# Four accumulators of an attention unit: the order of their matmuls in the first and the last pair of source blocks

## The chip, the cores and the metric

The kernel runs on one core of a Trainium2 chip. The metric is the device time of one execution in microseconds (us); lower is better. TensorE is called PE in the profile, VectorE DVE, ScalarE ACT, GpSimd POOL and SyncE SP.

## The reference

Four graph layers run one after the other over 4096 nodes with 64 features and one dense 0/1 adjacency. Each is wrapped as `x = x + layer(relu(layernorm(x)), adj, ...)`. The change lies in the first layer, a graph attention with eight heads of width 32. Its core is, cut to what matters:

```
mask = (adj > 0)
e    = leaky_relu(f1[:, None] + f2[None, :], 0.2)        # one per head
h    = elu(softmax(where(mask, e, -9e15)) @ Wh)          # 4096x4096 times 4096x32
```

Six heads are "spatial" (f1 and f2 come from the node features), two are "intent" heads (f1 and f2 come from an embedding). The heads' outputs are joined, multiplied by `W_out`, and a ninth attention of the same form follows; then the other three layers.

## The kernel before

**What a unit computes.** exp(leaky_relu(s + t)) takes one of two forms, by the sign of s + t, and each form is a product of a factor of the target and a factor of the source. So a head needs no exponential per edge: the kernel makes, for each edge, the flag "s + t is positive" (B) and "an edge where it isn't" (C), as bytes that TensorE reads as 8-bit floats, and sums the sources' scaled values over B and over C. A unit is one head over one half of the targets (2048 of 4096). There are 2 x 8 = 16 units, in the order of halves and, within them, of heads. They take the time from about 48 to 935 us of the profile.

**What a unit's loop does.** The 4096 sources are 32 blocks of 128; the loop at line 1552 and on takes them in 16 pairs. For each pair, `split_edges` makes the signs `st` of two blocks (line 1205 on ScalarE, or line 1199 on VectorE for a part of them), then B (line 1211, VectorE, an AND with the edges), then C (line 1219, VectorE, a XOR) where the pair is not "whole". In a whole pair the edges themselves take C's place, and B's share is taken off by a second set of matmuls with negated values `ycn`. The first and the last pair of a spatial unit are not whole; nor is the first pair of an intent unit.

**Accumulators.** Each product of one block is four matmuls, on four groups of 32 columns of TensorE, into four groups of 32 partitions of one accumulator (`add_up`, line 1541). The accumulators are PSUM tiles of 128 x 512 float32:

- accB: the values over B (two or three parts: a spatial head has one half-precision part here and its low part in accL; an intent head has three parts in accB)
- accL: the low part of a spatial head's values over B
- accD: the denominators over B
- accC: the values over C

accB and accC alternate between two pools from head to head (`ps_acc` and `ps_acc2`), so a unit's own pair of them is free while the one before is emptied. accL and accD are one tile each, in `ps_acc`: a unit can't write them before the unit before has been emptied.

**The end of a unit.** After the loop, eight small matmuls (line 1649) add a correction to accC, and then the four are emptied into `ev` (part of `h`): accD by VectorE (line 1657), accB by ScalarE (line 1658), accC by ScalarE (line 1659), and for spatial heads accL by VectorE (line 1661), which adds accL to what line 1658 has written and so waits for it. What follows from `ev` (`finish_unit`: transposes at line 1676, division, and after four heads the product with `W_out`) is put off to the third and fourth source block of the next unit.

**What sets the order.** The code issues the instructions in the order in which it is written, and the framework that compiles it places them into each engine's queue by priority (earlier in the code comes first) among those that its own estimate holds to be ready. So the queue's order is near the code's order and not the same. [...] B tiles are three deep, C and `st` tiles two deep. Inside a pair the code before emits, for each of the two blocks, accB, accL (spatial heads), accD; then for each block accC. In the first unit of each half (head 0) further matmuls into `dm` are tied behind the last of these products (`behind(sums)`), and in the very first unit the products of the other heads (`other_products`) too.

Of the kernel before, what the change touches and what calls it, by code (L numbers as in the profile page):

```python
# [26 lines left out]
NB = N // P  # L27
D = 64
G = 512
# [806 lines left out]
def kernel(  # L836
# [204 lines left out]
    with ExitStack() as l0:  # L1041
# [99 lines left out]
        def transfers_after(src, *pairs):  # L1141

            ins = nc.gpsimd.tensor_copy(tick.bitcast(src.dtype)[:, 0 : src.shape[1]], src)
            with tc.issue_after(ins.ins):
                for dst, s in pairs:
                    nc.gpsimd.dma_start(dst, s)
# [29 lines left out]
        @contextmanager  # L1176
        def behind(*marks):

            with ExitStack() as e:
                for i in marks:  # L1180
                    e.enter_context(tc.issue_after(i))
                yield
# [118 lines left out]
        with ExitStack() as pa:  # L1301
# [49 lines left out]
            with in_order():  # L1351
                nc.vector.tensor_reduce(fsum, FT[0:F, :], AX.X, ALU.add)
                for b0 in range(0, NB, 8):
                    pw = (ps, ps2)[b0 // 8 % 2].tile([P, 8, KZ], F32, name="pst", tag="misc")
                    for b in range(8):
# [4 lines left out]
                            start=True,  # L1360
                            stop=True,
# [50 lines left out]
                for k in range(2):  # L1412
                    pr = ps.tile([P, G], F32, name="prs", tag="misc")
                    for q in range(4):
# [5 lines left out]
                            start=True,  # L1420
                            stop=True,
# [23 lines left out]
        with ExitStack() as ha:  # L1445
# [27 lines left out]
            def load_products(zt, hd):  # L1473
                src = Z_d.rearrange("k p (h i) -> p k h i", h=NH - 1)[:, :, hd - 1, :]
                nc.sync.dma_start(zt.rearrange("p (k b) o -> p k (b o)", b=4), src)
# [4 lines left out]
            for hf in range(2):  # L1480
# [9 lines left out]
                for hd in range(NH):  # L1490
                    first = hd == 0
# [26 lines left out]
                    elif hf == 0 or hd + 1 < NH:  # L1518
# [6 lines left out]
                    spatial = hd < HS  # L1525
                    ycn = hp.tile([P, NB, 2 * O], F16, name="ycn", tag="ycn")
                    nc.vector.tensor_scalar(ycn, yc, -1.0, None, ALU.mult)
                    accB, accC = (
                        (ps_acc, ps_acc2)[hd % 2].tile([P, G], F32, name=n, tag=n)
                        for n in ("accB", "accC")  # L1530
                    )
                    accL, accD = (ps_acc.tile([P, G], F32, name=n, tag=n) for n in ("accL", "accD"))

                    parts = [(accB, yb[:, c]) for c in range(3)]
                    if spatial:
                        parts = [(a, yb[:, c].bitcast(F16)) for c, a in enumerate((accB, accL))]
                    parts.append((accD, yb[:, len(parts)]))

                    def add_up(acc, values, moving, start, stop):
                        for k in range(NS):  # L1540
                            ins = nc.tensor.matmul(  # L1541
                                acc[k * O : (k + 1) * O, :],
                                lhsT=values,
                                rhs=moving(k),
                                start=start,
                                stop=stop,
                            )
                        return ins.ins
# [3 lines left out]
                    for j0 in range(0, NB, 2):  # L1552
                        q = j0 // JT
                        t0 = j0 % JT
                        if spatial:
                            whole = j0 // 2 % 3 > 0
                        else:
                            whole = j0 // 2 % (5 if hf else 2) == 1
                        edges = mres[q][:, t0 : t0 + 2, :]
                        B, C = split_edges(  # L1560
                            epool,
                            srow,
                            nt[:, j0 : j0 + 2, hd],
                            edges,
                            j0 + hd * NB,
                            HEAD_STEPS[not spatial],
                            not whole,
                            3,
                        )
                        if whole:  # L1570
                            C = edges.bitcast(F8)
                        for i, j in enumerate(range(j0, j0 + 2)):
                            for n, (acc, y) in enumerate(parts):
                                sums = add_up(
                                    acc,
                                    y[:, j],
                                    lambda k, i=i: B[:, i, k * G : (k + 1) * G],
                                    start=j == 0 and (n == 0 or acc is not parts[n - 1][0]),
                                    stop=j == NB - 1 and (acc is not accB or n == len(parts) - 2 - spatial),
                                )  # L1580
                        for i, j in enumerate(range(j0, j0 + 2)):
                            for c in range(2):
                                cs = slice(c * O, (c + 1) * O)
                                add_up(
                                    accC,
                                    yc[:, j, cs],
                                    lambda k, i=i: C[:, i, k * G : (k + 1) * G],
                                    start=j == 0 and c == 0,
                                    stop=False,
                                )  # L1590
                                if whole:
                                    add_up(
                                        accC,
                                        ycn[:, j, cs],
                                        lambda k, i=i: B[:, i, k * G : (k + 1) * G],
                                        start=False,
                                        stop=False,
                                    )
                            if first:
                                with behind(sums):  # L1600
                                    add_up(
                                        dm,
                                        YD[:, j].rearrange("p c h -> p (c h)"),
                                        lambda k, q=q, j=j: mres[q].bitcast(F8)[
                                            :, j % JT, k * G : (k + 1) * G
                                        ],
                                        start=(j == 0),
                                        stop=(j == NB - 1),
                                    )
                        if hf == 0 and hd > 0 and j0 % (NB // 2) == 8 and later:  # L1610
                            transfers_after(B.bitcast(U8)[0:1, 0, 0:4], *later.pop(0))
                        if hf == 0 and first and j0 // 2 < NB // 4:
                            with behind(sums, *done_at):
                                other_products(j0 // 2)
                        if hf == 0 and first and j0 == NB // 2:
                            load_products(zt, hd + 1)
                        if j0 >= (NB // 2 + 4 if first else NB // 2 - 4):
                            with behind(*done_at):
                                for _ in range(2 if first else 1):
                                    next(coming, None)  # L1620
                        if j0 == 2 and pending:
                            pending()
                            pending = None
                    if first:
# [4 lines left out]
                        for b in range(GB):  # L1629
# [4 lines left out]
                                start=True,  # L1634
                                stop=True,
# [11 lines left out]
                    for c in range(2):  # L1647
                        for k in range(NS):
# [4 lines left out]
                                start=False,  # L1653
                                stop=c == 1,
# [254 lines left out]
        with ExitStack() as ob:  # L1909
# [185 lines left out]
            for u in range(4):  # L2095
                us = slice(u * HO2, (u + 1) * HO2)
                hs = slice((u % 2) * HO2, (u % 2 + 1) * HO2)
                accB, accC = (
                    [ps_acc.tile([P, G], F32, name="acco", tag="acc") for _ in range(NK)]
                    for _ in range(2)  # L2100
                )

                dd = ps_acc.tile([P, G], F32, name="ddo", tag="acc")
                for q in range(NQ):
# [11 lines left out]
                    for t in range(0, JT, 2):  # L2116
                        j0 = q * JT + t
                        edges = m[:, t : t + 2, :]
                        whole = j0 // 2 % 4 == 1
                        B, C = split_edges(  # L2120
                            work, srow[:, us], nto[:, j0 : j0 + 2], edges, j0, NB + 1, not whole, 4
                        )
# [6 lines left out]
                        for acc, Y, E in products:  # L2129
                            for i in range(2):  # L2130
                                for k in range(NK):
                                    sums = nc.tensor.matmul(
                                        acc[k],
                                        lhsT=Y[:, i].rearrange("p s d -> p (s d)"),
                                        rhs=E[:, i, k * G : (k + 1) * G],
                                        start=j0 + i == 0,
                                        stop=acc is accB and j0 + i == NB - 1,
                                    )
                    with behind(sums.ins):
                        for t in range(JT):  # L2140
                            j = q * JT + t
# [32 lines left out]
                for k in range(NK):  # L2174
# [4 lines left out]
                        start=False,  # L2179
                        stop=True,  # L2180
# [707 lines left out]
```

## Time and profile before

| | |
|---|---|
| median of 3 runs | 2041.64 us (2033.41 to 2043.93) |
| the profiled execution | 2039.13 us, of it 2037.1 us span |
| heads, 16 units | 48 to 935 us of the span |
| a unit in the second to the sixteenth place | 46 to 67 us, most 48 to 58 |
| TensorE's granted clock | mean 0.938 |

By units, from the changes of unit as the copies of accB show them (busy us of each engine; the first row is the unit of head 1 in the first half):

| stretch, us | length | PE | DVE | ACT | PE clock |
|---|---|---|---|---|---|
| 137 to 190 | 53 | 50.57 | 46.95 | 44.07 | 0.94 |
| 190 to 241 | 51 | 48.08 | 48.11 | 45.20 | 0.97 |
| 241 to 298 | 57 | 48.06 | 51.24 | 47.90 | 0.97 |
| 298 to 356 | 58 | 55.64 | 49.28 | 47.61 | 0.94 |
| 411 to 466 | 55 | 53.83 | 50.55 | 52.46 | 0.97 |
| 631 to 679 | 48 | 46.70 | 45.42 | 43.17 | 1.00 |
| 732 to 788 | 56 | 53.17 | 45.76 | 45.59 | 0.97 |
| 889 to 935 | 46 | 45.78 | 41.46 | 37.61 | 1.00 |

How to read it: a row of the profile's groups gives line, engine, operation, output and inputs, shape and count, then busy us and mean ns of one, and behind the second bar the engine's idle time just ahead of these instructions with what ended most of it. A row of the waits gives who waited for whom, the total us, how often, and the longest. A row of the timeline gives start, length, engine, line and operation, and in brackets the idle time ahead of it with its releaser. A row of the stretches gives the stretch, its length, each engine's busy time with its count of instructions (PE, PE's weight loads, DVE, ACT, POOL), the granted clock of TensorE, the DMA share and GB/s. The four matmuls of one product overlap, so their busy times are not a sum.

### The profile page before, as it was taken

To read this page: it belongs to the slowest core of one execution; us is meant where nothing else is said; L and a number is where in the kernel's file an instruction comes from. 1 tells how busy PE (TensorE), PEld (TensorE's weight loads), DVE (VectorE), ACT (ScalarE), POOL (GpSimd) and SP (SyncE) were. 2 spreads that over 40 slices of the span, in tenths; PEclk is the share of its full clock that TensorE was granted. 3 is DMA by queue.
4 is the path that set the end of the run, shared out by engine and by line. 5 is a ranking of instruction groups with operands and counts; after the bars stand their busy time and mean duration, and the time that the engine had idled before them with its cause. 6 is when DMAs were issued, how large, how long until landed. Compare 5 with 4: busy or idle time off the path is not lost. (4 is left out here: it accounts for less than half of the span.)

```text
span 2037.1 us, 44155 instructions
## 1 busy us (share of the span) xinstructions
PE 1815.8 (89%) x19323; PEld 821.8 (40%) x19340; DVE 1530.0 (75%) x2239; ACT 1476.9 (72%) x1439; POOL 83.3 (4%) x125
## 2 busy tenths in 40 slices
PE   5889989999999999996788958999999995789998
PEld 3444445444444444443234442333333333344332
DVE  5779988998789879996989867888788788533000
ACT  2768987899689878993778847777777753227676
POOL 2000100100000000001011100000000000000000
PEclk8899999999999999997899977999999996899999
DMA  9945555434211111103686406444344334412232
GB/s 112 178 115 99 100 99 72 164 118 172 86 49 49 48 49 54 54 2 125 254 276 227 163 17 235 137 145 143 124 140 140 124 134 151 152 63 70 91 99 64
DMA packets 117016, 239.05 MB, mean 117 GB/s; under 512 B 11062, under 2 KB 84006, under 8 KB 102054
## 3 DMA queue, kind: packets, MB, share of 16 engines
q1 hardware_dynamic: 101996, 192.95, 28.1%
q0 software_dynamic: 14816, 43.18, 11.8%
q8 instruction: 153, 2.51, 0.5%
q14 instruction: 51, 0.42, 0.1%
HBM read 245.37 MB, written 49.46 MB: 145 GB/s over the span
## 5 line engine op out<-in xcount | busy, mean ns | idle before, releaser
L1205 ACT ACTIVATE st<-srow,nt 128x2048 int8<-128x2048 f32 x352 | 682.8, 1994 | 78.9 <-DVE B L1211 78.1
L1211 DVE TENSOR_TENSOR B<-st,mres 128x1024 int32<-128x1024 int32 x256 | 311.7, 1220 | 70.5 <-PE accC L1541 46.6
L1541 PE MATMUL accB<-B,ybh 128*32 128x512 fp8e4 x3072 | 340.6, 384 | 13.3 <-DVE B L1211 13.3
L1541 PE MATMUL accD<-B,ybh 128*32 128x512 fp8e4 x2048 | 303.0, 388 | 23.0 <-DVE h L1657 23.0
L1541 PEld LDWEIGHTS <-ybh 128*32 128x32 bf16 (+1 forms) x6656 | 197.4, 98 | 236.8 <-issue 74.8
L1541 PE MATMUL accC<-mres,ych 128*32 128x512 fp8e4 x2272 | 269.2, 381 | 0.0
L1541 PE MATMUL accC<-B,ycn 128*32 128x512 fp8e4 x2272 | 269.0, 381 | 0.0
L1541 PE MATMUL accL<-B,ybh 128*32 128x512 fp8e4 x1536 | 221.6, 390 | 4.6 <-DVE h L1661 4.5
L1541 PEld LDWEIGHTS <-ych 128*32 128x32 f16 x4096 | 170.2, 99 | 116.1 <-issue 11.3
L1199 DVE TENSOR_SCALAR st<-srow,nt 128x2048 uint8<-128x2048 f32 x160 | 205.4, 1284 | 2.5
L2339 PE MATMUL accj<-sg,who 128*64 128x512 f32 (+1 forms) x512 | 197.8, 616 | 5.9 <-DVE sg L2332 5.5
L2339 PE MATMUL acci<-sg,who 128*64 128x512 f32 (+1 forms) x512 | 197.8, 616 | 0.0
L2295 ACT ACTIVATE yt<-pu,consts 128x512 f32<-128x512 f32 x144 | 98.7, 687 | 98.7 <-PE pu L2294 98.6
L2284 ACT ACTIVATE sg<-pl,rb 128x512 f32<-128x512 f32 x256 | 160.9, 679 | 8.2 <-PE pl L2279 5.2
L2771 ACT ACTIVATE w3b<-pv 128x1024 int16<-128x1024 f32 x128 | 131.0, 1024 | 42.4 <-PE pv L2762 41.2
L1205 ACT ACTIVATE st<-srowo,nto 128x1024 int8<-128x1024 f32 x128 | 138.3, 1138 | 25.0 <-DVE B L1211 24.9
L1541 PE MATMUL accC<-C,ych 128*32 128x512 fp8e4 x1824 | 149.3, 393 | 0.8 <-DVE C L1219 0.8
L955 DVE SCALAR_TENSOR_TENSOR raw<-raw 128x2048 f32<-128x2048 f32 x64 | 146.1, 2282 | 3.3 <-DMA raw<-in_adj_dram 3.3
L1219 DVE TENSOR_TENSOR C<-B,mres 128x1024 int32<-128x1024 int32 x114 | 139.5, 1225 | 3.6
L1541 PEld LDWEIGHTS <-ycn 128*32 128x32 f16 x2272 | 108.4, 97 | 62.7 <-issue 1.9
L2332 DVE SCALAR_TENSOR_TENSOR sg<-pf,sg 128x512 f32<-128x512 f32 x112 | 72.1, 685 | 38.9 <-PE pf L2329 38.9
L2778 DVE COPY ev<-sacc 128x512 f32<-128x512 f32 x4 | 2.8, 691 | 124.8 <-PE sacc L2736 124.8
(497 smaller groups left out, 2756.4 us busy)
## 6 DMA issues: line engine op xcount, KB each, us to landing
raw<-in_adj_dram SPq DMA_DIRECT2D x64, 1024.0 KB, 6.0
mo<-edges SPq DMA_DIRECT2D x32, 512.0 KB, 4.9
noedge<-nmo POOLq DMA_DIRECT2D x32, 512.0 KB, 4.3
nm<-noedge SPq DMA_DIRECT2D x64, 256.0 KB, 3.1
m<-edges SPq DMA_DIRECT2D x16, 1024.0 KB, 4.8
m<-edges SPq DMA_DIRECT2D x32, 512.0 KB, 3.8
srow<-srow_d SPq DMA_DIRECT2D x15, 1024.0 KB, 6.7
mres<-in_adj_dram POOLq DMA_DIRECT2D x8, 1024.0 KB, 35.4
```

What stands on the lines that cost most here:

```text
L955: nc.vector.scalar_tensor_tensor(raw, raw, 0.0, raw, ALU.is_gt, ALU.not_equal, accum_out=bad[:, c : c + 1])
L1199: nc.vector.tensor_scalar(st[:, i, :].bitcast(U8), srow, negs[:, i : i + 1], EDGE, ALU.is_gt, ALU.mult)
L1205: nc.scalar.activation(st[:, i, :], srow, AF.Sign, bias=negs[:, i : i + 1], scale=-1.0)
L1211: nc.vector.tensor_tensor(B.bitcast(I32), st.bitcast(I32), edges.bitcast(I32), ALU.bitwise_and)
L1219: nc.vector.tensor_tensor(C.bitcast(I32), B.bitcast(I32), edges.bitcast(I32), ALU.bitwise_xor)
L1541: ins = nc.tensor.matmul(acc[k * O : (k + 1) * O, :], lhsT=values, rhs=moving(k), start=start, stop=stop,)
L2284: nc.scalar.activation(sg[:, b0 + k, :], pl, AF.Sigmoid, bias=rb[:, j : j + 1], scale=1.0)
L2295: nc.scalar.activation(far[gi, gj][:, b, :], pu, AF.Sigmoid, bias=nb_t, scale=2.0 * DIST_K / (DIST_S * DIST_S),)
L2332: nc.vector.scalar_tensor_tensor(v[:, t, :], pf, F_K3, v[:, t, :], ALU.add, ALU.mult)
L2339: nc.tensor.matmul(acc[r : r + n, :], lhsT=XQ[:, src, cols], rhs=w, start=start, stop=stop)
L2771: nc.scalar.activation(w, pv, AF.Relu)
L2778: (nc.vector.tensor_copy if k % 2 else nc.scalar.copy)(ev[:, k, :], accs[k])
```

## The change

Inside the loop over pairs, the products over B are split into those into accB and those into the others (accL and accD). In the last pair of every unit, those into accL and accD of both blocks come first, then those into accB of both blocks, then accC as before. In the first pair of every unit but the two of head 0, those into accB of both blocks come first, then accC of both blocks, and those into accL and accD of both blocks last. All other pairs keep their order. The instructions themselves, their operands and their number stay as they are.

```diff
-                        for i, j in enumerate(range(j0, j0 + 2)):
-                            for n, (acc, y) in enumerate(parts):
-                                sums = add_up(
-                                    acc,
-                                    y[:, j],
-                                    lambda k, i=i: B[:, i, k * G : (k + 1) * G],
-                                    start=j == 0 and (n == 0 or acc is not parts[n - 1][0]),
-                                    stop=j == NB - 1 and (acc is not accB or n == len(parts) - 2 - spatial),
-                                )
+                        def inside(of_b):
+                            for i, j in enumerate(range(j0, j0 + 2)):
+                                for n, (acc, y) in enumerate(parts):
+                                    if (acc is accB) not in of_b:
+                                        continue
+                                    ins = add_up(
+                                        acc,
+                                        y[:, j],
+                                        lambda k, i=i: B[:, i, k * G : (k + 1) * G],
+                                        start=j == 0 and (n == 0 or acc is not parts[n - 1][0]),
+                                        stop=j == NB - 1
+                                        and (acc is not accB or n == len(parts) - 2 - spatial),
+                                    )
+                            return ins
+
+                        if j0 == NB - 2:
+                            inside([False])
+                            sums = inside([True])
+                        elif j0 == 0 and not first:
+                            sums = inside([True])
+                        else:
+                            sums = inside([True, False])
...
+                        if j0 == 0 and not first:
+                            inside([False])
                         if hf == 0 and hd > 0 and j0 % (NB // 2) == 8 and later:
```

## The prediction

> **What bounds the kernel now.** I read the page first: TensorE is the busiest engine, VectorE and ScalarE are close, and line 1541, which issues the products of the heads, holds the largest matmul rows.
>
> ```profile
> PE 1815.8 (89%) x19323; PEld 821.8 (40%) x19340; DVE 1530.0 (75%) x2239; ACT 1476.9 (72%) x1439; POOL 83.3 (4%) x125
> ...
> L1541 PE MATMUL accB<-B,ybh 128*32 128x512 fp8e4 x3072 | 340.6, 384 | 13.3 <-DVE B L1211 13.3
> L1541 PE MATMUL accD<-B,ybh 128*32 128x512 fp8e4 x2048 | 303.0, 388 | 23.0 <-DVE h L1657 23.0
> ```
>
> The idle time ahead of accD is not a lack of data: line 1657 is the copy that empties accD of the unit before. Then the waits of TensorE from 137 to 935 us, the heads after their first unit:
>
> ```profile
> PE accD L1541 <- DVE h L1657: 19.7, 10, 3.9
> PE pt L1676 <- DVE rd L1693: 7.4, 7, 2.1
> PE accL L1541 <- DVE h L1661: 4.5, 6, 3.3
> ```
>
> So 24.2 us of TensorE's time go to accD and accL. Then the timeline of one change of unit:
>
> ```profile
> 239.16 1.22 DVE L1219 TENSOR_TENSOR C<-B,mres 128x1024 int32<-128x1024 int32 x1
> ...
> 239.85 0.61 PE L1649 MATMUL accC<-em,meanq 32*32 32x512 f16 x8
> 240.31 1.28 DVE L1199 TENSOR_SCALAR st<-srow,nt 128x2048 uint8<-128x2048 f32 x1
> ...
> 240.39 0.40 PE L1541 MATMUL accB<-B,ybh 128*32 128x512 fp8e4 x4
> 241.50 1.22 DVE L1211 TENSOR_TENSOR B<-st,mres 128x1024 int32<-128x1024 int32 x1
> 241.57 0.56 ACT L1658 COPY h<-accB 128x512 f32<-128x512 f32 x1
> 242.64 0.68 DVE L1657 COPY h<-accD 128x512 f32<-128x512 f32 x1
> ...
> 243.24 0.68 DVE L1661 SCALAR_TENSOR_TENSOR h<-accL,h 128x512 f32<-128x512 f32 x1
> ...
> 244.07 0.62 PE L1541 MATMUL accL<-B,ybh 128*32 128x512 fp8e4 x4 [3.27 <-DVE h L1661]
> 244.44 0.67 PE L1541 MATMUL accD<-B,ybh 128*32 128x512 fp8e4 x4
> ```
>
> Line 1649 ends a unit. The next one issues its first four matmuls into accB (a "four" below: four matmuls on four groups of columns), then stands for 3.27 us until VectorE has come to the copies at 242.64 and 243.24. The C of the new unit's first pair was done at 240.38, and nothing used it. Last, the stretches behind three changes (TensorE's clock is the number after POOL):
>
> ```profile
> 243.00:247.00 4.00, 2.93 (x32) 1.36 (x36) 3.34 (x4) 4.00 (x3) 0.00 (x0) 0.57 0.41 44
> 298.00:305.00 7.00, 6.14 (x58) 2.53 (x61) 6.17 (x7) 6.80 (x6) 0.00 (x0) 0.51 0.24 98
> 632.00:636.00 4.00, 2.94 (x50) 1.29 (x46) 3.71 (x5) 2.77 (x3) 0.00 (x0) 1.00 0.86 316
> ```
>
> After long stalls the clock is near one half: in the timeline, fours start 0.43 us apart there and 0.216 us apart elsewhere. After the short stall at 632 (0.85 us) it stays at 1.00.
>
> **What the Trainium skill says.** "TensorE: Matmul & The Clock Gate", Part 1, "What's actually happening": an idle window of about 3.4 us takes the clock to half, a busy one takes it back. The trace agrees in size (half pace for about 3.4 us, at 298 for about twice that). The same page, Part 3, "The mechanism": matmuls start and end in queue order. The trace agrees: no accC product passed the waiting accL. The same page's "Architectural detail" calls VectorE's and ScalarE's queues strictly first in, first out. The trace shows copies behind whole operations, not the rule itself. "PSUM — Partial Sum Buffer", "Specifications (TRN2)": eight banks of 2 KiB. Two sets of accB and accC, one accD, one accL and two scratch tiles fill them, so accD and accL exist once; no trace shows a bank count.
>
> **The change, part by part.** No instruction is added or removed. *First pair of a unit (14 of 16; the two units of head 0 keep their order).* A spatial unit now has after the first four one more into accB and four into accC (its first pair isn't "whole"), before accL or accD is needed: 5 fours x 0.216 = 1.08 us. An intent unit had three fours into accB ahead of accD, and now six and four into accC: 7 x 0.216 = 1.51 us. Each is worth that or the stall, whichever is less. Stalls in the timeline at each change of unit: 142, 516, 586, 680 and 837: none with a release by lines 1657 or 1661; 188: 3.56; 240: 3.27; 294: 3.89 and 0.20; 356: 2.23 and 0.20; 407 (intent next): 2.83; 463 (intent): 0.80; 632: 0.85 and 0.21; 730: 2.61 and 0.41; 789: 0.86 and 0.21; 885 (intent): 1.72. Filled: 188, 240, 294, 356 and 730 5 x 1.08 = 5.40; 407 1.51; 463 0.80; 632 and 789 2 x 1.07 = 2.14; 885 1.51. Sum 11.4 us.
>
> *The clock.* Six changes are followed by half pace. The shortest stall with it is 2.23 us (356), the longest without 1.72 (885). What is left is 2.48, 2.19 and 2.8 at 188, 240, 294 (half pace stays), but 1.15, 1.32 and 1.5 at 356, 407, 730: it should go. Each 3.4 us at half pace costs 1.7: 3 x 1.7 = 5.1 us. Together 16.5 us of TensorE.
>
> *What it is worth in time.* A unit takes some 53 us, and VectorE is busy 47 to 51 of them in the first half of the heads. TensorE's gain shows only as far as VectorE waits for TensorE in the unit that follows; past that VectorE is late next. Waits of VectorE's line 1211, unit by unit, two of them:
>
> ```profile
> DVE B L1211 <- PE accC L1541: 0.5, 1, 0.5
> ...
> DVE B L1211 <- PE accC L1541: 6.4, 3, 3.0
> ```
>
> The first is the unit from 241, the second that from 298. Gain against wait (unexplained waits of that line counted with it): 190: 1.08 of 1.7; 241: 1.08 of 0.5; 298: 1.08 of 6.4; 356: 2.8 of 2.2; 411: 3.2 of 0.8; 466: 0.8 of 3.1; 631: 1.07 of 1.0; 732: 2.8 of 6.6; 788: 1.07 of 1.5; 889: 1.51 of 2.8 (its final wait for accD). The smaller of each: 1.08+0.5+1.08+2.2+0.8+0.8+1.0+2.8+1.07+1.51 = 12.8 us.
>
> *Last pair (all 16 units).* accD and accL now end two fours (0.43 us) sooner in a spatial unit, accD up to six (1.3 us) in an intent one; accB ends later by two fours in a spatial unit. At 240 accD had ended before the 239.85 of line 1649 and its copy ran at 242.64, behind one sign and one B: VectorE's queue decides, not the matmul. The framework orders each queue by its own estimate (the trace has accD ahead of accL at 358.58, against the code). So the copies can move a place either way: one sign (1.28 us) earlier for line 1657, or line 1658 one sign of ScalarE (2.00 us) later, and with it line 1661, which reads its result. Over about eight stalled changes that is from -10 to +16 us. I take 0: nothing read here says which. Nothing on the DMA queues moves: the marks at line 1143 follow B tiles of middle pairs, and the first pair's B is let go behind accL and accD as before.
>
> **Sum.** The profiled execution took 2039.1 us (span 2037.1 and 2.0 around it): 2039.1 - 12.8 = 2026.3. The median shown is 2.5 us higher: 2028.8, taken as 2028.
>
> **Rivals.** *Copies move up.* Lines 1657 and 1661 come one VectorE operation earlier as well. Then most stalls go, and all six spells of half pace (about 12 us): TensorE gains near 30, of which VectorE's waits on it let pass some 24: 2018. For: accD ends before line 1649 and the copy has three operations to pass. Against: B of the next pair has its inputs early and keeps its place.
> *Hidden.* VectorE and ScalarE are the bound in more units than I count (ScalarE waited 70.7 us for line 1211, a loop of the two), and TensorE idles elsewhere: gain 0 to 5, 2039. Also here: the framework issues other products in the gap, so that the change doesn't give the order it names. For: units 241 and 411; against: 6.4 and 6.6 us of waits on TensorE at 298 and 732.
> *Slower: accB ends last.* Line 1658 falls behind one more sign (2.00 us) in the ten changes where the next unit uses accL. Then accL comes 2.0 later and 1.08 of it is filled: 10 x 0.92 = 9, and four changes now warm (586, 632, 680, 789) fall to half pace, 4 x 1.7 = 7: 2058. It decides once line 1661 moves back by more than 1.08 us in most changes. For: in the timelines lines 1658 and 1661 stand close together at 294 (1661 waits for it at 407). Against: elsewhere line 1658 is done over a microsecond before 1661.
>
> **How the numbers follow.** Forecast (2020 to 2034) 0.42; copies move up (2008 to 2020) 0.18; hidden (2034 to 2046) 0.18; slower (2046 to 2066) 0.22. The likeliest is 2028. A measurement here can tell about 0.5% (10 us) from no change: faster is below 2031.4, so 0.34 of the first and all of the second, 0.52. Slower is above 2051.8, 0.20. The rest, 0.28, is the same. The range takes the second case whole and the slower one to 2056, leaving under 2 in 10 out; the likeliest case's own is 2020 to 2034.
>
> **What would show it.** accC's products between accB's and accD's at each change; idle ahead of accD and accL down from 24.2 to about 13 us; clock near 1.00 behind 356, 407 and 730; VectorE's waits for accC down. I am wrong if line 1661 or 1658 stands further back in its queue, if idle time ahead of accB on line 1211 grows by what accD's loses, or if accC waits for line 1219.

## The result, and the profile after

The changed kernel takes 2049.02 us (median of 22 runs, 2039.97 to 2054.79), against 2040.62 us for the kernel before (22 runs): a ratio of 1.0043, 95% interval 1.0029 to 1.0058. That is 8.4 us slower, less than the 0.5% named ahead, but its interval is clear of no change. Timed once more beside the experiments it gave 2048.39 us and 1.0042 (1.0026 to 1.0059). The forecast, 2028, had the sign wrong.

The page's engine line, and the rows of the products into accD and accL (output and inputs, count, busy us, mean ns, then the idle time ahead of them and its releaser):

```profile
PE 1816.4 (89%) x19340; PEld 815.6 (40%) x19340; DVE 1529.9 (75%) x2239; ACT 1477.2 (72%) x1439; POOL 83.3 (4%) x125
...
L1541 PE MATMUL accD<-B,ybh 128*32 128x512 fp8e4 x2048 | 288.5, 390 | 0.0
...
L1541 PE MATMUL accL<-B,ybh 128*32 128x512 fp8e4 x1536 | 211.8, 391 | 24.0 <-DVE h L1676 24.0
```

The work is the same. The idle time ahead of accD is gone, and ahead of accL stand 24.0 us. Before, the same rows had 23.0 and 4.6 us; of these 24.2 lay behind 137 us, so that from there on the sum has stayed as it was. (In the changed file the copies that empty the accumulators stand fifteen lines lower: 1672 accD, 1673 accB, 1676 accL, 1691 the transposes.) TensorE's waits in the same part of the heads:

```profile
PE accL L1541 <- DVE h L1676: 24.0, 8, 4.6
PE pt L1691 <- DVE rd L1708: 14.6, 9, 3.7
PE pf L1645 <- ACT h L1641: 6.6, 2, 5.1
```

The longest single wait for accL is 4.6 us, where it was 3.3; the transposes of the follow-up work wait twice as long as before (14.6 against 7.4). The stretch of the heads from 137 us, in the changed kernel:

```profile
137.30:937.40 800.10, 751.25 (x12807) 369.07 (x12811) 706.03 (x776) 683.71 (x419) 25.52 (x33) 0.98 0.30 78
```

TensorE is idle for 48.9 us of it (800.10 - 751.25); in the kernel before it is idle for 41.3 us of the same stretch (its row stands under "First pair only"). The change of unit that the prediction showed at 240 us, in the timeline after:

```profile
242.25 0.61 PE L1664 MATMUL accC<-em,meanq 32*32 32x512 f16 x8
242.71 1.28 DVE L1199 TENSOR_SCALAR st<-srow,nt 128x2048 uint8<-128x2048 f32 x1
...
242.80 0.62 PE L1541 MATMUL accB<-B,ybh 128*32 128x512 fp8e4 x8
...
243.24 1.04 PE L1541 MATMUL accC<-C,ych 128*32 128x512 fp8e4 x16
243.90 1.22 DVE L1211 TENSOR_TENSOR B<-st,mres 128x1024 int32<-128x1024 int32 x1
245.04 0.68 DVE L1672 COPY h<-accD 128x512 f32<-128x512 f32 x1
245.15 2.00 ACT L1205 ACTIVATE st<-srow,nt 128x2048 int8<-128x2048 f32 x1 [1.09 <-DVE B L1211]
245.64 1.21 DVE L1211 TENSOR_TENSOR B<-st,mres 128x1024 int32<-128x1024 int32 x1
246.89 1.29 DVE L1199 TENSOR_SCALAR st<-srow,nt 128x2048 uint8<-128x2048 f32 x1
247.06 0.57 ACT L1673 COPY h<-accB 128x512 f32<-128x512 f32 x1
...
248.09 0.68 DVE L1676 SCALAR_TENSOR_TENSOR h<-accL,h 128x512 f32<-128x512 f32 x1
...
248.83 0.62 PE L1541 MATMUL accL<-B,ybh 128*32 128x512 fp8e4 x4 [4.55 <-DVE h L1676]
249.23 0.64 PE L1541 MATMUL accD<-B,ybh 128*32 128x512 fp8e4 x4
```

The new first pair does what was meant: five more fours run ahead of the stall (accB x8, accC x16). But the stall behind them is 4.55 us, where 2.2 were forecast. Before, the copies of accD and accL followed each other in VectorE's queue (242.64 and 243.24), and the next B came behind them. Now a B and a sign stand between them (245.64 and 246.89). It is so at ten of the twelve changes that have a copy of accL, all but the two behind head 0. The copy of accB, whose result the copy of accL reads, stands one sign of ScalarE further back: 4.8 us behind the start of line 1664's matmuls, before 1.7 (241.57 against 239.85).

By stage: from the start of the first product into accB to that of the last matmul of line 1649 (its new place is line 1664) the heads took 876.1 us before, and 881.2 and 880.6 in the two profiles of the changed kernel: 4.8 us more on the mean. Counted from the end of the first unit it is 3.0 and 4.9 us, for the first product starts at another moment in each profile. The instructions behind the heads stand in the same order in both kernels.

### The profile page after: what moved, and what is told of

Same layout as the page of the kernel before. It is cut to its first block, busy times and chain, and to the rows that moved or that the text cites. A ratio compares the mean times of both kernels' runs of the same rounds, so it can differ in the third digit from the quotient of the medians.

```text
span 2050.2 us, 44180 instructions
## 1 busy us (share of the span) xinstructions
PE 1816.4 (89%) x19340; PEld 815.6 (40%) x19340; DVE 1529.9 (75%) x2239; ACT 1477.2 (72%) x1439; POOL 83.3 (4%) x125
## 3 DMA queue, kind: packets, MB, share of 16 engines
q0 software_dynamic: 14816, 43.18, 11.7%
## 5 line engine op out<-in xcount | busy, mean ns | idle before, releaser
L1541 PE MATMUL accB<-B,ybh 128*32 128x512 fp8e4 x3072 | 326.1, 386 | 14.4 <-DVE B L1211 14.4
L1541 PE MATMUL accD<-B,ybh 128*32 128x512 fp8e4 x2048 | 288.5, 390 | 0.0
L1541 PE MATMUL accC<-mres,ych 128*32 128x512 fp8e4 x2272 | 264.3, 381 | 0.0
L1541 PE MATMUL accC<-B,ycn 128*32 128x512 fp8e4 x2272 | 263.8, 380 | 0.0
L1541 PE MATMUL accL<-B,ybh 128*32 128x512 fp8e4 x1536 | 211.8, 391 | 24.0 <-DVE h L1676 24.0
L1541 PEld LDWEIGHTS <-ych 128*32 128x32 f16 x4096 | 162.7, 98 | 116.0 <-issue 8.6
L1541 PE MATMUL accC<-C,ych 128*32 128x512 fp8e4 x1824 | 144.9, 387 | 1.4 <-DVE C L1219 1.4
L1541 PEld LDWEIGHTS <-ycn 128*32 128x32 f16 x2272 | 103.8, 97 | 62.5 <-issue 2.2
L2147 PE MATMUL acco<-B,YBo 128*128 128x512 fp8e4 x256 | 71.5, 401 | 28.8 <-DVE B L1211 28.7
```

The lines of the kernel that those rows point to most:

```text
L1541: ins = nc.tensor.matmul(acc[k * O : (k + 1) * O, :], lhsT=values, rhs=moving(k), start=start, stop=stop,)
L2147: sums = nc.tensor.matmul(acc[k], lhsT=Y[:, i].rearrange("p s d -> p (s d)"), rhs=E[:, i, k * G : (k + 1) * G], start=j0 + i == 0, stop=ac ...
```

## The experiments

Three theories were put to the chip first. Theory Q: the loss comes from the last pair. accB now ends last, so the copy of accB, and with it that of accL, falls back in its queue. Rival P: the loss comes from the first pair. Rival H: VectorE and ScalarE set the length of the heads whatever TensorE's order is. "Half pace" below is time in which TensorE's granted clock was 0.50, added up over the heads from the clock's record in the trace. Half of it is lost, by the prediction's starts of fours (0.43 us apart and 0.216).

The first four, each against the kernel before in the same set of runs:

| kernel | median, us | ratio to before, 95% interval | heads, us | waits for accD / accL, us |
|---|---|---|---|---|
| before | 2039.21 | 1 | 876.1 | 19.7 / 4.5 |
| first pair only | 2036.16 | 0.9984 (0.9968 to 1.0000) | 871.8 | 1.5 / 12.2 |
| last pair only | 2046.08 | 1.0033 (1.0016 to 1.0050) | 882.0 | 12.3 / 14.0 |
| first pair, accB first in the last | 2036.71 | 0.9993 (0.9978 to 1.0009) | 871.0 | 1.7 / 12.5 |
| change, copies pinned | 2038.26 | 0.9987 (0.9969 to 1.0005) | 871.5 | 0.0 / 12.1 |

The waits are TensorE's, from 137 us to the end of the heads. The heads are from one profile each, so they lean on one execution; the ratio does not.

**First pair only.** The order of the first pair as in the change, the last pair as before. In the trace VectorE and ScalarE then work in the order of before up to the copies, at every change of unit; behind them the negation `ycn` comes one or more operations earlier in at least four units.

```diff
-                        if j0 == NB - 2:
-                            inside([False])
-                            sums = inside([True])
-                        elif j0 == 0 and not first:
+                        if j0 == 0 and not first:
                             sums = inside([True])
```

> The new order in the first pair alone; the last pair as before, so VectorE's and ScalarE's queues stay in the order of before. Theory Q (the loss comes from the copy of accL, which the new last pair puts one B and one sign further back in VectorE's queue): TensorE's waits for the copies of accD and accL fall from 24.2 us to about 13, the half pace behind 356, 407 and 730 us goes, and the time is 8 to 16 us under before, near 2028. Rival P (the loss comes from the first pair: accL and accD last hold its B longer, and VectorE waits for accD): slower than before, 2045 to 2050, with VectorE's wait for accD at 13 us as in the changed kernel. Rival H (VectorE and ScalarE bound the heads, the rest is chance in the clock behind them): within 3 us of before.

2036.16 us, 0.9984: the sign is theory Q's, the size is not, and the interval reaches 1. Rival P is out, as this isn't slower; the time alone fits rival H as well. The waits for accD and accL fell from 24.2 to 13.7 us, 10.5 less, as worked out (11.4), but the time fell by 3. Where it went, TensorE's waits in this kernel:

```profile
PE pt L1688 <- DVE rd L1705: 16.4, 10, 3.3
PE accL L1541 <- DVE h L1673: 12.2, 7, 3.1
PE pf L1642 <- ACT h L1638: 6.6, 2, 5.1
```

The transposes of the follow-up work, two pairs later, wait 9.0 us longer for VectorE than before (7.4). So nearly all that was filled came back as another wait, and TensorE's idle time stayed as it was. The stretch from 137 us, in the kernel before and in this one:

```profile
137.00:934.10 797.10, 755.84 (x12808) 374.92 (x12811) 706.53 (x776) 683.50 (x419) 25.55 (x34) 0.97 0.30 78
```

```profile
137.00:929.90 792.90, 751.69 (x12807) 370.74 (x12811) 706.80 (x776) 683.34 (x419) 25.53 (x34) 0.98 0.30 78
```

TensorE is idle for 41.3 us before (797.10 - 755.84) and for 41.2 here; what became shorter is the busy time, of which 3.4 us less half pace explain 1.7. The wait for `pf` (2.7 us before, 6.6 here) is no further loss: it holds the stall of the first change of unit, which lies just ahead of 137 us and was left out of the 24.2. Before, and in this kernel:

```profile
135.85 0.40 PE L1541 MATMUL accD<-B,ybh 128*32 128x512 fp8e4 x4 [3.36 <-DVE h L1657]
...
138.31 1.92 PE L1630 MATMUL pf<-fold_f,h 128*128 128x32 f32 x8 [1.87 <-ACT h L1626]
```

```profile
138.29 1.92 PE L1642 MATMUL pf<-fold_f,h 128*128 128x32 f32 x8 [5.14 <-ACT h L1638]
```

VectorE's timeline behind one change of unit shows why the transposes wait; here the kernel before, and below it this one:

```profile
789.78 0.68 DVE L1657 COPY h<-accD 128x512 f32<-128x512 f32 x1
790.38 0.68 DVE L1661 SCALAR_TENSOR_TENSOR h<-accL,h 128x512 f32<-128x512 f32 x1
790.98 1.22 DVE L1211 TENSOR_TENSOR B<-st,mres 128x1024 int32<-128x1024 int32 x1
792.48 1.23 DVE L1211 TENSOR_TENSOR B<-st,mres 128x1024 int32<-128x1024 int32 x1 [0.28 <-issue]
...
797.82 0.20 DVE L1691 TENSOR_REDUCE rd<-pt 128x16 f32<-128x48 f32 x1
```

```profile
786.16 0.68 DVE L1669 COPY h<-accD 128x512 f32<-128x512 f32 x1
786.76 0.68 DVE L1673 SCALAR_TENSOR_TENSOR h<-accL,h 128x512 f32<-128x512 f32 x1
787.36 2.52 DVE L1211 TENSOR_TENSOR B<-st,mres 128x1024 int32<-128x1024 int32 x2
...
793.98 0.20 DVE L1703 TENSOR_REDUCE rd<-pt 128x16 f32<-128x48 f32 x1
```

From the copy of accD to the first reduction behind the transposes VectorE takes 8.04 us before and 7.82 here: but for 0.28 us before, it works back to back in both. Of a stall of 1.07 us in this place 0.38 are left, and the unit became 0.4 us shorter; the transposes wait 0.90 us here, and waited 0.24 before. (The profile puts the 0.90 down to a sign of ScalarE, so that it isn't in the 16.4; the operation of VectorE on `rd` that ended the 0.24 ends here at 794.41, 0.04 us before the transposes go on.)

Not all that VectorE lost is work. In the second half of the heads it stands until the load of `ych`, which the negation `ycn` reads, has landed; before this was one wait of 1.9 us, here it is:

```profile
DVE ycn L1527 <- DMA ych<-YC_d: 4.9, 2, 3.1
```

**Last pair only.**

```diff
-                        elif j0 == 0 and not first:
-                            sums = inside([True])
...
-                        if j0 == 0 and not first:
-                            inside([False])
```

> The new order in the last pair alone; the first pair as before. Theory Q: the copy of accL stands as far back as in the changed kernel and nothing fills the wait, so TensorE waits 30 to 40 us for the copies and the time is 10 to 20 us over before, slower than the changed kernel. Rival P: no slower than before, 2036 to 2041. Rival H: within 3 us of before.

2046.08 us, 1.0033: 6.9 us slower, and heads longer by 5.9. Its queues of VectorE and ScalarE have the copies where the changed kernel has them. The waits:

```profile
PE accL L1541 <- DVE h L1672: 14.0, 8, 2.8
PE accD L1541 <- DVE h L1668: 12.3, 9, 2.6
```

26.3 us, 2.1 more than before, and not the 30 to 40 expected: in this kernel accD's products are placed ahead of accL's and run in between, so that part of the lateness of accL is filled. The time beyond these 2.1 us is not in these rows: the transposes waited 10.9 us against 7.4, and half pace in the heads was 52.1 us against 48.9, worth 1.6. The expected range of the time (10 to 20 us) was too high as well. Rivals P and H are out for this part: both had it at no loss.

**accB first in the last pair.** The new first pair, and in the last pair accB ahead of accL and accD.

```diff
                         if j0 == NB - 2:
-                            inside([False])
                             sums = inside([True])
+                            inside([False])
```

> The new first pair, and in the last pair accB of both blocks first, then accL and accD: the copy of accB, which the copy of accL waits for, can start sooner. Theory Q: the copies of accD and accL follow each other in VectorE's queue, TensorE's waits for them are 10 to 14 us, the time is 8 to 16 us under before, like the first pair alone. Rival P: about as slow as the changed kernel, 2045 to 2050. Rival H: within 3 us of before.

2036.71 us, 0.9993: the loss is gone, as theory Q has it; a gain isn't shown, where 8 to 16 us were expected. The queue of VectorE again has the copies next to each other. Rival P is out, for the new first pair is in this kernel.

**The change with the copies pinned.** TensorE's products are emitted as in the changed kernel; two further orders hold the copies ahead of their neighbours.

```diff
-                        B, C = split_edges(
+                        with behind(*(emptied[0:1] if j0 == 6 else ())):
+                            B, C = split_edges(
...
+                                emptied[1:] if j0 == 4 else (),
...
-                    nc.scalar.copy(ev[:, 1, :], accB)
+                    emptied = [nc.scalar.copy(ev[:, 1, :], accB).ins]
```

(`emptied` holds the copies of accB and accL of the unit before; its second entry is put ahead of B of the next unit's third pair, its first ahead of the signs of the fourth.)

> The whole change, with B of the next unit's third pair held behind the copy of accL in VectorE's queue and the signs of its fourth pair behind the copy of accB in ScalarE's. TensorE's order is that of the changed kernel. Theory Q: the waits for accL shrink from 24.0 us to 12 to 16, the time comes to 2026 to 2036, under before. Rival P: no change against the changed kernel, 2045 to 2050. Rival H: within 3 us of before.

2038.26 us, 0.9987. The same place in its timeline:

```profile
240.41 1.22 DVE L1212 TENSOR_TENSOR B<-st,mres 128x1024 int32<-128x1024 int32 x1
240.48 0.56 ACT L1677 COPY h<-accB 128x512 f32<-128x512 f32 x1
241.55 0.68 DVE L1676 COPY h<-accD 128x512 f32<-128x512 f32 x1
...
242.15 0.68 DVE L1681 SCALAR_TENSOR_TENSOR h<-accL,h 128x512 f32<-128x512 f32 x1
...
242.89 0.40 PE L1543 MATMUL accL<-B,ybh 128*32 128x512 fp8e4 x4 [2.10 <-DVE h L1681]
```

The accumulators end in the order of the changed kernel, the copy of accL comes 0.60 us behind that of accD, and the stall is 2.10 us instead of 4.55. (At eight of the ten changes a sign still stands between the two copies.) The time misses the 2026 to 2036 expected, and a gain over before isn't shown, but the loss is gone. So it is the place of the copies in the two queues that costs the 8 us, not the order of the products as such; both queues were pinned at once, so which of the two costs how much stays open. This settles the loss. It left a second question: why was the first pair worth 3 us and not 13? Theory V: VectorE's work sets the pace behind a change of unit. Rival T: the transposes stand badly in TensorE's queue. Rival K: chance in the clock behind the heads hides a gain. The runs on it, with the kernel before in the same set:

| kernel | median, us | ratio to before, 95% interval | heads, us | half pace in the heads, us |
|---|---|---|---|---|
| before | 2039.88 | 1 | 876.1 | 48.9 |
| before, no negation | 2028.82 | 0.9932 (0.9909 to 0.9955) | 865.3 | 27.6 |
| first pair, no negation | 2023.26 | 0.9924 (0.9899 to 0.9949) | 860.2 | 31.5 |
| first pair, negation on GpSimd | 2100.06 | 1.0292 (1.0267 to 1.0317) | 931.6 | 89.7 |
| first pair, finish later | 2033.45 | 0.9967 (0.9953 to 0.9981) | 865.3 | 24.6 |

**No negation.** `ycn` is 16 VectorE operations, 11 us. Two kernels leave it out, one with the first pair's order and one with that of before; B's share in whole pairs is then added and not taken off, so that the sums are not the reference's:

```diff
-                    ycn = hp.tile([P, NB, 2 * O], F16, name="ycn", tag="ycn")
-                    nc.vector.tensor_scalar(ycn, yc, -1.0, None, ALU.mult)
+                    ycn = yc
```

> The new first pair alone, and the negation of the values (ycn, 16 VectorE operations of 0.69 us) left out: the products over B in whole pairs then take the values themselves, so the second form's sums are not the reference's; matmuls are as many as before. Theory V (VectorE's back-to-back work sets the pace behind a change of unit, so that what TensorE fills comes back as a wait for VectorE): the heads shorten by 6 to 11 us against the first pair alone, to about 2026 to 2031. Rival T (the wait of the transposes, as placed in TensorE's queue, eats the gain): 0 to 3 us, about 2035. Rival K (chance in the clock behind the heads hid a gain): no effect of its own, 2036.

> The kernel before with the negation of the values left out (second form's sums not the reference's). Theory V: 6 to 11 us under before, 2029 to 2034, for the order before is bound by VectorE as well; the difference to the first pair with the negation left out stays near 3 us. Rival T: within 3 us of before. Rival K: within 3 us of before.

2023.26 and 2028.82 us. The heads became 11.6 us shorter than in the first pair alone, and 10.8 shorter than before: about as many as the 11 us taken off VectorE, in both orders. That is theory V's; T and K had next to nothing. The stretch of the heads in the kernel before with the negation taken out of it, to be read against the 797.10 us above:

```profile
136.40:919.80 783.40, 748.10 (x12810) 374.27 (x12811) 699.12 (x762) 683.25 (x419) 24.39 (x34) 0.98 0.30 79
```

VectorE's count in the stretch falls by 14 (776 to 762; the first two of the 16 operations, at 67.9 and 123.6 us, lie ahead of it) and its busy time by 7.4 us, but the stretch by 13.7. Two other things went with the negation. Half pace fell by 21.3 us, which is itself worth some 10.7 us of TensorE. And VectorE's waits for the load of `ych` went, 1.9 us before and 4.9 in the first pair alone: the two units in which the first pair alone had them give 8.4 of the 11.6 us. VectorE's time, the clock and these waits can't be told apart by this pair of runs: a VectorE that comes sooner leaves shorter stalls, and these leave the clock up.

**Negation on GpSimd.**

```diff
-                    nc.vector.tensor_scalar(ycn, yc, -1.0, None, ALU.mult)
+                    nc.gpsimd.tensor_scalar(ycn, yc, -1.0, None, ALU.mult)
```

> The new first pair alone, with the negation of the values moved from VectorE to GpSimd, which is idle for most of the heads. Theory V: as with the negation left out, 2026 to 2033, if GpSimd has it done before the second pair needs it and doesn't slow VectorE. Rival T and rival K: 2034 to 2037.

2100.06 us, 63.9 us slower than the first pair alone. The row of the groups, and one place of the timeline:

```profile
L1527 POOL TENSOR_SCALAR ycn<-ych 128x2048 f16<-128x2048 f16 x16 | 92.8, 5800 | 442.2 <-DMA ych<-YC_d 314.8 <-PE pt L1688 56.5 <-DVE ych L1279 48.3
```

```profile
236.98 7.18 DVE L1199 TENSOR_SCALAR st<-srow,nt 128x2048 uint8<-128x2048 f32 x1
...
237.68 5.39 POOL L1527 TENSOR_SCALAR ycn<-ych 128x2048 f16<-128x2048 f16 x1
...
244.07 1.20 DVE L1211 TENSOR_TENSOR B<-st,mres 128x1024 int32<-128x1024 int32 x1
...
245.33 0.62 PE L1541 MATMUL accB<-B,ybh 128*32 128x512 fp8e4 x4 [5.60 <-DVE B L1211]
```

One negation takes 5.8 us where VectorE took 0.69, and VectorE is held up meanwhile: the sign beside it takes 7.18 us where it takes 1.28 elsewhere, and TensorE waits 5.60 us for the B behind it. It is so at all 16: beside each an operation of VectorE takes 2 to 6 us longer than its like in the first pair alone, 64 us in sum. So the condition that the expectation named ("doesn't slow VectorE") failed, and the run shows theory V the other way round: though it no longer does the negation, VectorE was busy 51.7 us longer than in the first pair alone (1582.6 against 1530.9, whole kernel), and the heads became 59.8 us longer. Half pace rose as well, to 89.7 us, so that the clock has a part in it.

**Finish later.** The follow-up work begun behind the fourth pair of the next unit, in the first pair's order.

```diff
-                        if j0 == 2 and pending:
+                        if j0 == 6 and pending:
```

> The new first pair alone, with the follow-up work of the unit before (finish_unit: transposes, division) begun behind the fourth pair and not behind the second. Theory V: VectorE has as much to do, so within 4 us of the first pair alone (2036); the wait of the transposes shrinks and waits for B or C grow. Rival T: the waits of the transposes for VectorE (16.4 us in the first pair alone) fall to below 6 and the time falls by 8 to 12 us, to 2024 to 2028. Rival K: 2036.

2033.45 us: within the 4 us that theory V gave it, and not the 8 to 12 of rival T. The transposes' waits did not shrink (21.1 us against 16.4), so T falls; they wait for VectorE in this place too. Yet it is the first complete kernel that is clearly faster than before, which V did not foresee. The heads are 6.5 us shorter than in the first pair alone; half pace is 20.9 us less, worth 10.4, while TensorE's idle time from 137 us on rose from 41.2 to 44.4 us. So what it gained is the clock.

**Finish later in the order of before; the negated values by DMA; the change again.** The first of these changes that one line in the kernel before. The second adds to the "finish later" kernel a store of `ycn` in the first half of the targets and a load in the second, which takes 8 operations off VectorE:

```diff
+                    if hf == 0:
...
+                        nc.sync.dma_start(YN_d[hd].rearrange("p (b c) -> p b c", b=NB), ycn)
+                    else:
+                        ycn = negated
...
+                        nc.sync.dma_start(
+                            negated, YN_d[(hd + 1) % NH].rearrange("p (b c) -> p b c", b=NB)
+                        )
```

> The kernel before with the follow-up work behind the fourth pair and nothing else. If the later place is worth something of its own, 3 us under before, near 2037; if it only let the first pair's order pay, no faster than before (2039 to 2042).

> The first pair's new order, the follow-up work behind the fourth pair, and the negated values stored in the first half of the targets and loaded in the second, which takes eight operations of 0.69 us off VectorE. Theory V: 5 to 6 us under the same kernel without that (2033), near 2028, and faster than both kernels. If VectorE is not the bound in the second half: 2033 or more, for 8 MB more of transfers.

> The changed kernel once more, beside the runs of the parts. If the two parts add up: first pair -3 and last pair +7 give about +4 us over before, 2044. If they hinder each other, as the first timing of it had it: +8, 2048 to 2049.

Against 2039.36 us for the kernel before in these runs: finish later alone 2044.11, 1.0022 (1.0011 to 1.0034); with the first pair and the negated values by DMA 2032.10, 0.9956 (0.9940 to 0.9972); the change again 2048.39. So the later place alone loses, and with the first pair's order (2033.45 us, above) it gains. The heads of these two are 880.7 and 865.3 us, and half pace is 47.9 and 24.6 us: 23.3 us less half pace is worth 11.7 us of TensorE, most of the 15.4 us between them. Why the clock holds in the one and not in the other was not tried. The DMA version took 3.6 us off the second half of the heads against "finish later" (415.6 to 412.0, 5 to 6 us were expected in all), gave 3.0 back in the first half, and its median is only 1.4 us lower, inside the intervals. It is faster than both kernels all the same, as is "finish later".

## Why the prediction was wrong

**The stall, and what fills it: right, with one stall missed.** The products moved ahead of accD and accL as worked out; taken alone, the first pair lowers their waits from 137 us on by 10.5 us, and 11.4 were forecast. The prediction's list has no stall at the first change (142 us); there was one of 3.36 us, at 135.85, and filling it gained nothing, for `pf` behind it starts at the same time as before.

**What it is worth in time: the first term that failed.** The forecast took, unit by unit, the smaller of TensorE's gain and VectorE's wait for TensorE, 12.8 us. The runs gave 3 us (0 to 6.5). A wait of VectorE on line 1211 elsewhere in a unit is not spare time for the copies at the unit's end. These stand among operations which run back to back, so TensorE meets VectorE again at the transposes, two pairs on; it waited there 9.0 us longer, and its idle time from 137 us on was 41.2 us, before 41.3. In the second half of the heads, where 6.4 us had been credited, the units behind 632, 730, 789 and 885 became 0.2, 0.9, 0.4 and 0.1 us shorter. That VectorE sets this pace rests on these waits and on the two runs which gave VectorE less and more to do; the clock moved with them in both, so this cause is in part argued.

**The clock: mostly not.** Half pace was to go behind three changes, 5.1 us. In the first pair alone it fell by 3.4 us of spell in all, 1.7 us of time (48.9 to 45.5): it went behind 298, 356 and 407, stayed behind 730, and came elsewhere, as behind transposes that had waited 2.48 us (413.64). In the changed kernel it did go behind 356 and 407 at once, and came elsewhere: 49.0 us, the same. The forecast went by the length of the stalls at changes of unit, with a border between 1.72 and 2.23 us. In the trace of before a wait of 2.14 us at the transposes, 526.03 us, has half pace behind it too, and in the changed kernel the clock stays at 1.00 behind a stall of 3.83:

```profile
526.70:530.10 3.40, 3.40 (x26) 1.35 (x26) 1.50 (x4) 2.89 (x2) 0.00 (x0) 0.50 0.02 5
```

```profile
305.16 0.40 PE L1541 MATMUL accL<-B,ybh 128*32 128x512 fp8e4 x4 [3.83 <-DVE h L1676]
```

```profile
304.00:311.00 7.00, 5.84 (x90) 2.98 (x91) 6.36 (x10) 5.89 (x5) 0.18 (x1) 1.00 0.01 5
```

So the length alone doesn't decide, and a stall need not fill the idle window of which the prediction speaks; what else decides was not tried.

**The last pair: the second term that failed, and the one with the sign.** The prediction set it to 0, within -10 and +16, because "nothing read here says which". It measured +6.9 us alone (1.0033), with the move that the prediction had named as a sign of being wrong. Line 1661 reads what line 1658 writes, and accB now ends two fours later; line 1658 falls behind one more sign of ScalarE, and a B of the next unit goes into VectorE's queue ahead of line 1661. Line 1657 did move up by one sign at eight of ten changes, as the rival "copies move up" had it; line 1661 moved back by one B there, and by a B and a sign at the other two (240 and 679 us). That line 1661 waits for line 1658 could be read from the code of before; which way the queues would turn could not.

**The rivals.** "Slower: accB ends last" is what happened, in mechanism; its 2058 was nearly twice the measured loss, for it counted ten changes at 0.92 us and four new spells of half pace; the first profile has eight waits for accL, and behind the four changes named no half pace at once (the second has it behind 586, as the kernel before had). "Copies move up" and "hidden" were each half right, the first for the copy of accD, the second for the first pair.

**What stays open.** The two parts alone give -3 and +7, near +4, and together +8.4; the intervals of the sum and of the whole overlap. Counted from the end of the first unit, the heads say +2.1 for the sum and +3.0 and +4.9 for both together. So that the parts hinder each other isn't shown. If they do, it could be because the changed kernel has accL ahead of accD in TensorE's queue, so that accD's earlier copy helps nobody; no run tried that. The rest of the 8.4 us should lie behind the heads, in code that is the same: there the two profiles of the changed kernel are 9.8 and 3.1 us longer than that of before, with 18.2 and 11.0 us more half pace, worth 9.1 and 5.5. The kernel with the copies pinned, which isn't slower by its median, is 8.4 us longer there in its profile, so one profile can't show a loss in this part.

## What to carry to other kernels

When an engine stands waiting for a copy, look first at what the copying engine does: if it works back to back up to that copy and beyond, work moved into the stall can return as a wait for the next thing it delivers. To see whether it did, compare the idle time of the waiting engine over the whole stage, not that of one wait. Price a reordered product by when its consumers may be queued as well as by its own engine: in a chain of two copies in two engines' queues the second goes back with the last product that feeds the first. If an order of products needs its copies in a certain place, pin that place, rather than trust that it comes with the order.

## What the runs showed of the hardware that was not expected

The negation of 128 x 2048 half-precision values took 5.8 us on GpSimd and 0.69 us on VectorE, and while GpSimd worked on it, VectorE was held: a sign beside it took 7.18 us where it takes 1.28, and all 16 negations together held VectorE for 64 us. Half pace of TensorE can weigh as much as the change that is measured: two kernels that differ in one line (the place of the follow-up work, in the first pair's order) had 45.5 and 24.6 us of it in the heads. A stall of 3.83 us was followed by full clock in one kernel, and waits of 2.1 us by half pace in another. Of each kernel that ran twelve times or more, the runs spread over 11 to 22 us, with the same program.
